# A graph layer with two feed-forward blocks: where a constant is added, which queue carries six stores, and what is done ahead of a branch

## The chip, the cores and the metric

The kernel runs on one core of a Trainium2 chip. The metric is the device time of one execution in microseconds. The core has five engines with an instruction stream each: TensorE (PE; its weight loads are shown as PEld), VectorE (DVE), ScalarE (ACT), GpSimd (POOL) and SyncE (SP), which here only issues transfers. Transfers are issued by SP, by POOL (all gathers, and in the change a few stores) and at the start by ACT. Engines and transfers wait for each other through semaphores.

## The reference

The input is x of 6250 nodes by 256, and 100,000 edges (src, dst), sorted by dst. Four residual blocks follow one another, each on the layer norm of x:

```python
x = x + gnn0(layernorm(x), W1, W2, b, src, dst)          # messages t1[src] + (f[src]*f[dst]) @ W2, summed by dst
x = x + ffn0(layernorm(x), wr, br, w1, b1, w2, b2)       # top half of the nodes by x @ wr gets gelu(x@w1+b1)@w2+b2, times that weight
x = x + gnn1(layernorm(x), edge_index, W, att_src, att_dst, bias, W_res, ...)
x = x + ffn1(layernorm(x), Wr, br, W1, b1, ..., Wo, bo)  # 8 experts of two layers with batch norm, all computed, mixed by a softmax
```

The change lies around gnn1, which is an attention over the edges into each node:

```python
xn = layer_norm(x, ln1_g, ln1_b)
h = (xn @ W).reshape(N, 8, 32)
e = leaky_relu((h*att_src).sum(-1)[src] + (h*att_dst).sum(-1)[dst], 0.2)
ee = exp(e - segment_max(e, dst)[dst]);  denom = segment_sum(ee, dst)
agg = segment_sum(h[src] * (ee / denom[dst])[:, :, None], dst)
out = layer_norm(agg + xn @ W_res + bias, ln2_g, ln2_b)
return out + gelu_tanh(out @ ffn_w1 + ffn_b1) @ ffn_w2 + ffn_b2
```

Adding out to x means adding (normed * ln2_g + ln2_b), and the ffn's bias ffn_b2 is a constant per column as well. The kernel holds ln2_b + ffn_b2 as one row, `cst`.

## The kernel before, in words

The 6250 nodes are 50 tiles of 125 rows (NT, NP). x stays in SBUF for the whole run as X. The edges of each tile, sorted by dst, are cut into slices of 128; each tile has 17 slices (SL) plus one place for the tile's own rows (the self loops), in three groups of six (GS, NG). The indices of all slices lie in sdT, as source rows (srcT) and as local destinations (dloc). A copy of the local destinations in DRAM, dltab, is read with a broadcast over the partitions to make the transposed one-hot matrices ohT (535.5 KB for a tile).

**First pass**, up to about 1246 us: gnn0 and ffn0, interleaved by generators. ffn0 (L519 to 545) works on chunks of four tiles (the last two chunks are of two and of one tile, 47, 48 and 49); each tile's result y goes from PSUM through DVE to SBUF and by `ndma` (L80 to 87, two transfers of 112 and 13 rows) to ytab in DRAM. L537 calls it. By the time of the last two chunks, `select` is at work: it finds the top half of the nodes by a search on DVE (L1342 to 1348), the routing. roots_of "rb" (rs, L178 to 185) makes the last reciprocal roots. On SP, the next transfer after the y stores is the load of h_w1 (L162), then h_w2, ohT0 (L680) and ten loads of Y, which bring ytab back (L85). They stand in this order in SP's stream.

**Between the passes.** For each tile, a list of steps (L784 to 792) does on staggered tiles: X += Y * wm (L784, DVE, both inputs in SBUF), norm to z (L742 on DVE for one tile in three, L744 on ACT), two transposes (L750), the gain (L754 on ACT, L755 on DVE), the product with W and the attention columns (L760) and the eviction (L777). Groups of five tiles are stored to htab, 264 columns wide: 256 of h and 8 attention terms. Then POOL gathers the rows of the first four groups of edges into a ring of four buffers, `ring` (fetch_edges, L699), by an indirect transfer per slice (L208). A loop over pairs of tiles (L848 to 865), here called the W_res loop, makes xn @ W_res, adds g_bias on DVE and stores rows to rtab, four tiles at a time. Among its steps, from t = 10 on, one step each of terms_by_parts (L829 to 845) builds adsh: the destination's attention term and its shift, split into three bf16 parts.

Then comes a branch (L866 to 880): a value is read from SBUF to all engines, and a general path is taken if the shifts are too far apart; with these inputs it is not taken. Every engine passes it.

**Second pass.** Its engines PE, DVE and ACT follow an order written out by hand, POOL and SP are ordered by the scheduler. Groups s = 0 to 149 (three a tile) go through four quarters:

- spread (L903): six matmuls of ohT with adsh give pa, the destination's terms per edge.
- quarter0 (L936): DVE reduces pa to ad and makes w (L941 to 945).
- quarter1 (L956): ACT takes exp of w into the group's rows (L959); DVE makes lo = rows − hi of the group before (L964).
- quarter2 (L966): fetch of a further group, spread of the next, and DVE multiplies the rows by the weights (L976, two halves).
- quarter3 (L978): PE sums rows by destination with the one-hot oh, in the two parts hi and lo (L986); ACT makes hi (L996), DVE makes oh (L998).

tile_end (L913) divides by the sum of weights and adds rr, the W_res row loaded from rtab (fetch_tile, L889 to 897, which also loads ohT of the tile; onehot_t, L899 to 901, compares it). own_rows (L691) loads the tile's own rows of htab.

The tiles are then taken in 14 chunks (1, 2, 3 and eleven times 4 tiles) through the norm, the ffn (up L1059, down L1070) and the experts (L1157, L1175, L1178). `run` shares the quarters of the next chunk's tiles out among the current chunk's matmuls. add_o (L1046 to 1053) is three POOL instructions for each chunk: o *= ln2_g, X += cst, X += o. The middle one needs nothing of the chunk but X as it is after L784, and in the trace all fourteen of it run between 1248 and 1317 us, among the products h.

The start of the second pass in the source (L1274 to 1284): fetch_tile(0), the own rows of the four ring buffers, the first experts' weights (`load`: W and Wo, L162), spread(0), then the quarters of the first chunk, among which fetch_tile(1) and fetch_tile(2) are called.

Of the kernel before, what the change touches and what calls it, by code (L numbers as in the profile page):

```python
# [9 lines left out]
F32 = mybir.dt.float32  # L10
# [4 lines left out]
ALU = mybir.AluOpType  # L15
# [45 lines left out]
def gnn_ffn(ctx, tc, A, out):  # L61
# [17 lines left out]
    def ndma(sb, tab, t0, load, eng=None):  # L79

        eng = eng or nc.sync
        view = tab[NP * t0:NP * (t0 + sb.shape[1]), :].rearrange("(t p) d -> p t d", p=NP)
        for a, b in ((0, SPLIT), (SPLIT, NP)):
            if load:
                eng.dma_start(sb[a:b], view[a:b])  # L85
            else:
                eng.dma_start(view[a:b], sb[a:b])
# [327 lines left out]
    with ExitStack() as p1:  # L415
# [103 lines left out]
        def ffn0(t0, c):  # L519
            xT = made.pop(t0)  # L520
            n = c * NP
            hT = []
            for f in range(NF):
                ph = psum.tile([P, CT * NP], F32, name="ph")
                for k in range(KD):
                    nc.tensor.matmul(ph[:, 0:n], f_w1[:, k, f * P:(f + 1) * P], xT[:, k, 0:n], start=(k == 0), stop=(k == KD - 1))  # L526
                h = late.tile([P, CT * NP], F32, name="hT", bufs=NF + 1)
                nc.scalar.activation(h[:, 0:n], ph[:, 0:n], AF.Gelu_apprx_tanh, bias=f_b1[:, f:f + 1])
                hT.append(h)
                yield  # L530
            for j in range(c):
                y = late.tile([NP, 1, D], F32, name="y")
                py = psum.tile([NP, D], F32, name="py", bufs=1)
                for f in range(NF):
                    nc.tensor.matmul(py, hT[f][:, j * NP:(j + 1) * NP], f_w2[:, f, :], start=(f == 0), stop=(f == NF - 1))  # L535
                nc.vector.tensor_tensor(y[:, 0, :], py, f_b2[0:NP, :], ALU.add)
                ndma(y, ytab, t0 + j, False)  # L537
                t = t0 + j
                x2 = late.tile([NP, D], F32, name="x2", bufs=1)
                nc.vector.scalar_tensor_tensor(x2, y[:, 0, :], wts[:, t:t + 1], X[:, t, :], op0=ALU.mult, op1=ALU.add)  # L540
                bn(late, mv2[:, 1, t, :], x2)
                yield
            if t0 < CHUNKS0[-2][0]:
                roots_of(t0, t0 + c, "ra")
# [166 lines left out]
    with ExitStack() as md:  # L711
# [133 lines left out]
                        nc.vector.tensor_tensor(rem[:, ts], rem[:, ts], adsh[0:NP, ts, q, :], ALU.subtract)  # L845


        rr = None  # L848
        made_terms = terms_by_parts()
        for t in range(0, NT, 2):  # L850
            pr = psum.tile([NP, 2, D], F32, name="pr")
            for i in range(2):
                for k in range(KD):
                    nc.tensor.matmul(pr[:, i, :], xTs[t + i][:, k, :], wcat[:, k, HA:HA + D], start=(k == 0), stop=(k == KD - 1))
            j = t % 4
            if j == 0:
                rr = pool.tile([NP, 4, D], F32, name="rr")
            nc.vector.tensor_tensor(rr[:, j:j + 2, :], pr, g_bias[0:NP, None, :].to_broadcast([NP, 2, D]), ALU.add)
            if j == 2 or t + 2 == NT:
                ndma(rr[:, 0:j + 2, :], rtab, t - j, False)  # L860
            if t >= 10:
                next(made_terms, None)
        for _ in made_terms:
            pass
        mid.close()
        gen1 = nc.values_load(f1I[0:1, 0:1], min_val=0, max_val=1)  # L866
        with tc.If(gen1 > 0):
# [14 lines left out]
    with ExitStack() as p2:  # L882
# [6 lines left out]
        def fetch_tile(t):  # L889
            if t >= NT:  # L890
                return
            ohT = ohT0 if t == 0 else pool.tile([NP + 1, SL, P], BF16, name="ohT")
            if t:
                nc.sync.dma_start(ohT.rearrange("p i e -> p (i e)"), flat_ap(dltab, t * SL * P, [[0, NP + 1], [1, SL * P]]))
            rr = pool.tile([NP, 1, D], F32, name="rr")
            ndma(rr, rtab, t, True)
            tiles[t] = {"ohT": ohT, "rr": rr}
# [37 lines left out]

        def quarter0(s):  # L936

            if s < LAST:
                L = live[s]
                ad = pool.tile([P, GS, 2 * HEADS], F32, name="ad")  # L940
                nc.vector.tensor_reduce(ad, L["pa"].rearrange("p i q c -> p i c q"), AX.X, ALU.add)  # L941
                w = pool.tile([P, GS, HEADS], F32, name="w")
                nc.vector.tensor_tensor(w, L["rows"][:, :, D:], ad[:, :, 0:HEADS], ALU.add)
                nc.vector.scalar_tensor_tensor(w, w, 0.2, w, op0=ALU.mult, op1=ALU.max)
                nc.vector.tensor_tensor(w, w, ad[:, :, HEADS:], ALU.subtract)
                L["w"] = w
            if s >= 2 and (s - 1) % NG == 0:
                tile_end((s - 1) // NG - 1)
            if s >= 2 and (s - 1) % NG == 0:
                fetch(s + len(ring) - 2)  # L950
            if s >= 1 and (s - 1) % NG == 0:
                fetch_tile((s - 1) // NG + 1)
            if s + 1 < LAST and (s + 1) % NG == 0:
                onehot_t((s + 1) // NG)

        def quarter1(s):  # L956

            if s < LAST:
                nc.scalar.activation(live[s]["rows"][:, :, D:], live[s].pop("w"), AF.Exp)  # L959
            if 1 <= s <= LAST:  # L960
                L = live[s - 1]
                L["lo"] = pool.tile([P, GS, HW], F32R, name="lo", bufs=1)
                for c in halves(real(s - 1)):
                    nc.vector.scalar_tensor_tensor(L["lo"][:, c], L["rows"][:, c], 1.0, L["hi"][:, c].bitcast(F32), op0=ALU.mult, op1=ALU.subtract)  # L964

        def quarter2(s):  # L966

            if s >= 1 and s % NG != 0:
                fetch(s + len(ring) - 1)
            if s + 1 < LAST:  # L970
                spread(s + 1)
            if s < LAST:
                rows = live[s]["rows"]
                for c in halves(GS):
                    h4 = rows[:, c, 0:D].rearrange("p i (h j) -> p i h j", j=HD)
                    nc.vector.tensor_tensor(h4, h4, rows[:, c, D:, None].to_broadcast([P, GS // 2, HEADS, HD]), ALU.mult)  # L976
# [69 lines left out]
        def add_o(ci):  # L1046

            t0, n = CHUNKS1[ci]
            o = outs.pop(ci)[0]
            bc = [NP, n, D]  # L1050
            nc.gpsimd.tensor_tensor(o[:, 0:n, :], o[:, 0:n, :], ln2_g[0:NP, None, :].to_broadcast(bc), ALU.mult)
            nc.gpsimd.tensor_tensor(X[:, t0:t0 + n, :], X[:, t0:t0 + n, :], cst[0:NP, None, :].to_broadcast(bc), ALU.add)
            nc.gpsimd.tensor_tensor(X[:, t0:t0 + n, :], X[:, t0:t0 + n, :], o[:, 0:n, :], ALU.add)

        def up(ci, f):
# [216 lines left out]
            return 4 * NG * (t0 + n) + 4  # L1272

        fetch_tile(0)  # L1274
        for k in range(len(ring)):
            own_rows(k)
        load(0, ("W1", "W2", "Wo"))
        load(1, ("W1", "W2"))
        spread(0)
        advance(ends(0))  # L1280
        for ci in range(len(CHUNKS1)):
            t0, n = CHUNKS1[ci]
# [426 lines left out]
```

## Time and profile before

| | |
|---|---|
| median of three runs | 3138.24 us (3135.61 to 3140.74) |
| profiled execution | 3140.49 us, its span 3138.7 us, mean TensorE clock 0.949 |
| TensorE busy | 2786.7 us, 89% of the span |
| VectorE, ScalarE, GpSimd busy | 2081.0, 1170.0 and 1964.4 us |
| transfers | 407.55 MB, 130 GB/s in the mean |

Where the time lies, by windows of the trace:

| stage | us from the span's start | length | PE busy | DVE busy | POOL busy |
|---|---|---|---|---|---|
| end of routing, first loads of Y | 1232 to 1248 | 16 | 3.4 | 12.1 | 0.6 |
| products h, 50 tiles | 1248 to 1323 | 75 | 66.5 | 63.3 | 31.1 |
| first gathers, W_res loop | 1323 to 1376 | 53 | 45.1 | 27.6 | 22.3 |
| branch passed, first groups | 1376 to 1394 | 18 | 7.2 | 14.6 | 9.9 |
| first chunks | 1394 to 1750 | 356 | 306.5 | 292.8 | 252.3 |
| chunks of four, the period repeats | 1750 to 3004 | 1254 | 1246.6 | 971.9 | 791.7 |
| last chunk | 3004 to 3138 | 134 | 128.0 | 28.2 | 4.7 |

How such a table is read: a share of busy time says which engine sets the pace of a stage only if it is near the whole. In other stages the rows in order of time tell more. Such a row has the start, the duration, the engine, the line, the operation, output and inputs, the shape, how many instructions it sums up, and in brackets the idle time ahead of it and what ended it. "SPq" is SP issuing transfers.

### The profile page before, as it was taken

What the parts mean: (1) busy time and instruction counts of PE and PEld (TensorE: products, weight loads), DVE (VectorE), ACT (ScalarE), POOL (GpSimd) and SP (SyncE); (2) the same over time, 40 slices, a digit from 0 to 9 for tenths busy, and PEclk for the clock granted to TensorE, in tenths of its full rate; (3) what the DMA queues carried; (4) which work ended last, traced back from release to release, by engine and by line L of the source; (5) the groups of instructions that cost most, each with busy time, mean ns of one, the idle gap of its engine ahead of it and who ended that gap; (6) DMA issues with size and microseconds to landing.
All of it is one profiled execution on the core that took longest, in us unless ns stands there. A gap on an engine that the chain in (4) does not pass through costs nothing.

```text
span 3138.7 us, 40435 instructions
## 1 busy us (share of the span) xinstructions
PE 2786.7 (89%) x12748; PEld 1981.1 (63%) x12748; DVE 2081.0 (66%) x5836; ACT 1170.0 (37%) x2149; POOL 1964.4 (63%) x1752
## 2 busy tenths in 40 slices
PE   4358888888888896867899999999999999999999
PEld 4345666666666675656776666666666666666665
DVE  7744555555555547767888777877877778787731
ACT  3302222222222222615545455354554545445332
POOL 4677777777777760456777666666666666666400
PEclk8778999999999997978999999999999999999999
DMA  5453343433333333465664545545455454544412
GB/s 124 100 150 102 113 115 112 112 112 112 112 112 113 112 105 90 134 189 166 189 168 137 166 135 144 154 127 163 131 155 146 134 163 123 162 139 136 128 50 61
DMA packets 262809, 407.55 MB, mean 130 GB/s; under 512 B 55312, under 2 KB 202236, under 8 KB 262543
## 3 DMA queue, kind: packets, MB, share of 16 engines
q0 software_dynamic: 80000, 221.18, 25.9%
q1 hardware_dynamic: 172765, 173.98, 18.9%
q10 hardware_dynamic: 9810, 9.60, 1.2%
q8 instruction: 106, 1.74, 0.2%
q14 instruction: 128, 1.05, 0.1%
HBM read 371.33 MB, written 34.04 MB: 129 GB/s over the span
## 4 chain that ended last, share of the span: by engine, by line
PE 47%; DVE 6%; ACT 1%; issue 1%; DMA 1%; POOL 0%; DVEq 0%; SPq 0%; ACTq 0%; POOLq 0%
PE ph L1157 19%; PE py L1175 9%; PE iotaP L986 5%; PE py L1070 5%; PE ph L1059 5%; DVE hrow L976 1%; PE mi L1032 1%; PE mi L1097 1%; DMA hrow<-htab,sdT 1%; DVE lo L964 1%; PE pa L909 1%; DVE oh L998 0%; DVE bnst L190 0%; POOL hrow L208 0%; ACT hi L996 0%
## 5 line engine op out<-in xcount | busy, mean ns | idle before, releaser
L208 POOL DMA_INDIRECT hrow<-htab,sdT x850 | 1017.2, 1197 | 527.6 <-issue 220.8
L208 POOL DMA_INDIRECT rows<-gtab,sdT x800 | 758.5, 948 | 243.6 <-issue 132.5
L1158 ACT ACTIVATE h<-ph,bi,sc 128x500 f32<-128x500 f32 (+3 forms) x448 | 321.5, 723 | 538.2 <-PE ph L1157 538.0
L455 PE MATMUL ps<-rows,oh 128*125 128x257 f32 x1600 | 429.8, 414 | 64.8 <-DMA rows<-gtab,sdT 49.1
L455 PEld LDWEIGHTS ps<-rows,oh 128*125 128x125 f32 x1600 | 313.3, 203 | 178.5 <-DMA rows<-gtab,sdT 83.8
L1157 PE MATMUL ph<-h,W 128*128 128x500 f32 (+3 forms) x896 | 372.0, 548 | 0.0
L1175 PE MATMUL py<-Wo,h 128*125 128x256 f32 x1600 | 369.8, 381 | 0.4 <-ACT h L1158 0.4
L1157 PE MATMUL ph<-wcat,W 128*128 128x500 f32 (+3 forms) x896 | 363.9, 545 | 2.4 <-ACT h L1158 2.3
L1175 PEld LDWEIGHTS py<-Wo,h 128*125 128x125 f32 x1600 | 296.7, 188 | 72.2 <-issue 27.9
L976 DVE TENSOR_TENSOR hrow<-hrow 128x768 f32<-128x768 f32 x300 | 280.1, 974 | 70.8 <-ACT hrow L959 70.8
L1178 DVE SCALAR_TENSOR_TENSOR X<-py,gate,X 125x256 f32<-125x256 f32 x400 | 173.4, 477 | 203.3 <-PE py L1175 203.2
L964 DVE SCALAR_TENSOR_TENSOR lo<-hrow,hi 128x792 fp32r<-128x792 f32 (+1 forms) x300 | 286.9, 997 | 0.2 <-issue 0.2
L996 ACT ACTIVATE hi<-hrow 128x792 fp32r<-128x792 f32 (+1 forms) x300 | 236.2, 822 | 127.0 <-DVE hrow L976 122.9
L986 PE MATMUL iotaP<-hi,oh 128*125 128x264 f32 x850 | 251.9, 329 | 0.0
L1157 PEld LDWEIGHTS ph<-wcat,W 128*128 128x128 f32 x896 | 160.8, 192 | 140.3 <-issue 109.8
L1157 PEld LDWEIGHTS ph<-h,W 128*128 128x128 f32 x896 | 160.0, 194 | 106.3 <-issue 95.8
L986 PE MATMUL iotaP<-lo,oh 128*125 128x264 f32 x850 | 219.5, 291 | 5.1 <-DVE lo L964 5.0
L1059 PE MATMUL ph<-xT,h_w 128*128 128x500 f32 (+3 forms) x448 | 185.9, 556 | 4.6 <-ACT hT L1061 3.6
L526 PE MATMUL ph<-xT,f_w 128*128 128x500 f32 (+3 forms) x448 | 185.6, 539 | 0.0
L535 PE MATMUL py<-f_w,hT 128*125 128x256 f32 x800 | 182.9, 381 | 0.9
L1070 PE MATMUL py<-h_w,hT 128*125 128x256 f32 x800 | 177.6, 380 | 0.0
L986 PEld LDWEIGHTS iotaP<-lo,oh 128*125 128x125 f32 x850 | 162.4, 191 | 20.8 <-issue 7.6
(355 smaller groups left out, 3929.7 us busy)
## 6 DMA issues: line engine op xcount, KB each, us to landing
W<-in_L_ffn_W SPq DMA_DIRECT2D x224, 256.0 KB
Wo<-in_L_ffn_Wo SPq DMA_DIRECT2D x112, 256.0 KB
ohT<-dltab SPq DMA_DIRECT2D x50, 535.5 KB
hrow<-htab,sdT POOLq DMA_INDIRECT x850
rows<-gtab,sdT POOLq DMA_INDIRECT x800
hrow<-htab SPq DMA_DIRECT2D x50, 115.5 KB
X<-in_x ACTq DMA_DIRECT2D x10, 560.0 KB
ytab<-y SPq DMA_DIRECT2D x50, 112.0 KB
```

The source lines that it names most:

```text
L208: nc.gpsimd.indirect_dma_start(out=dst, out_offset=None, in_=tab, in_offset=bass.IndirectOffsetOnAxis(ap=idx, axis=0))
L455: nc.tensor.matmul(ps, oh[:, i, :], edge_rows[i], start=(s0 + i == 0), stop=(s0 + i == SL - 1))
L526: nc.tensor.matmul(ph[:, 0:n], f_w1[:, k, f * P:(f + 1) * P], xT[:, k, 0:n], start=(k == 0), stop=(k == KD - 1))
L964: nc.vector.scalar_tensor_tensor(L["lo"][:, c], L["rows"][:, c], 1.0, L["hi"][:, c].bitcast(F32), op0=ALU.mult, op1=ALU.subtract)
L976: nc.vector.tensor_tensor(h4, h4, rows[:, c, D:, None].to_broadcast([P, GS // 2, HEADS, HD]), ALU.mult)
L986: nc.tensor.matmul(tiles[t]["ps"], L["oh"][:, i, :], r[:, i, :], start=(g + i + q == 0), stop=(g * GS + i == SL - 1 and q == 1))
L996: nc.scalar.activation(L["hi"][:, c], L["rows"][:, c], AF.Copy)
L1059: nc.tensor.matmul(ph[:, 0:n], h_w1[:, k, f * P:(f + 1) * P], C["xT"][:, k, 0:n], start=(k == 0), stop=(k == KD - 1))
L1070: nc.tensor.matmul(py[:, i, :], C["hT"][f][:, j * NP:(j + 1) * NP], h_w2[:, f, :], start=(f == 0), stop=(f == NF - 1))
L1157: nc.tensor.matmul(ph[:, 0:n], w[:, k, f * P:(f + 1) * P], rhs[:, k, 0:n], start=(k == 0), stop=(k == KD - 1))
L1158: nc.scalar.activation(h[:, f, 0:n], ph[:, 0:n], AF.Relu, bias=cols[1][:, f, e:e + 1], scale=cols[0][:, f, e:e + 1])
L1175: nc.tensor.matmul(py[:, i, :], hidden[u, "2"][:, k, j * NP:(j + 1) * NP], weights[u, "Wo"][:, k, :], start=(k == 0), stop=(k == KD - 1))
```

## The change

There are four parts.

1. The y stores of the last two chunks of ffn0, tiles 47, 48 and 49, six transfers, are issued by POOL rather than by SP.
2. In add_o, cst is added to o rather than to X. There are as many instructions of the same size, but the middle one now depends on the chunk's o. In the changed program the fourteen stand in POOL's stream in their chunks, behind o *= ln2_g, and X += o comes behind them, with a gather between each two.
3. Group 0 of the edges is spread, weighed and multiplied among the steps of the W_res loop (at t = 38, 42 and 46), ahead of the branch; the quarters of s = 0 skip these steps. The terms start one step sooner (t = 8), and none are left after the loop. The pa of group 0 takes one of the PSUM buffers "mi".
4. fetch_tile(1) follows fetch_tile(0), ahead of the own rows and of the weights on SP, rather than in the first quarters.

```diff
-                ndma(y, ytab, t0 + j, False)
+                ndma(y, ytab, t0 + j, False, eng=nc.gpsimd if t0 >= CHUNKS0[-2][0] else None)
...
+        def spread_first():
+            pa = psum.tile([P, GS, 3, 2 * HEADS], F32, name="mi", bufs=3)
+            for i in range(GS):
+                nc.tensor.matmul(pa[:, i].rearrange("p q c -> p (q c)"), ohT0[:, i, :], adsh[:, 0].rearrange("p q c -> p (q c)"),
+                                 start=True, stop=True)
+            hts["pa"] = pa
+
+        def weigh_first():
+            rows = ring[0]
+            ad = wp.tile([P, GS, 2 * HEADS], F32, name="ad0")
+            nc.vector.tensor_reduce(ad, hts.pop("pa").rearrange("p i q c -> p i c q"), AX.X, ALU.add)
+            w = wp.tile([P, GS, HEADS], F32, name="w0")
+            nc.vector.tensor_tensor(w, rows[:, :, D:], ad[:, :, 0:HEADS], ALU.add)
+            nc.vector.scalar_tensor_tensor(w, w, 0.2, w, op0=ALU.mult, op1=ALU.max)
+            nc.vector.tensor_tensor(w, w, ad[:, :, HEADS:], ALU.subtract)
+            nc.scalar.activation(rows[:, :, D:], w, AF.Exp)
+
+        def multiply_first():
+            rows = ring[0]
+            for c in (slice(0, GS // 2), slice(GS // 2, GS)):
+                h4 = rows[:, c, 0:D].rearrange("p i (h j) -> p i h j", j=HD)
+                nc.vector.tensor_tensor(h4, h4, rows[:, c, D:, None].to_broadcast([P, GS // 2, HEADS, HD]), ALU.mult)
+
+        firsts1 = {38: spread_first, 42: weigh_first, 46: multiply_first}
...
-            if t >= 10:
+            if t >= 8:
                 next(made_terms, None)
-        for _ in made_terms:
-            pass
+            if t in firsts1:
+                firsts1[t]()
+        assert next(made_terms, 0) == 0
...
-            if s < LAST:
+            if 0 < s < LAST:
                 L = live[s]
                 ad = pool.tile([P, GS, 2 * HEADS], F32, name="ad")
...
-            if s < LAST:
+            if 0 < s < LAST:
                 nc.scalar.activation(live[s]["rows"][:, :, D:], live[s].pop("w"), AF.Exp)
...
-            if s < LAST:
+            if 0 < s < LAST:
                 rows = live[s]["rows"]
...
-            if s >= 1 and (s - 1) % NG == 0:
+            if s > 1 and (s - 1) % NG == 0:
                 fetch_tile((s - 1) // NG + 1)
...
-            nc.gpsimd.tensor_tensor(X[:, t0:t0 + n, :], X[:, t0:t0 + n, :], cst[0:NP, None, :].to_broadcast(bc), ALU.add)
+            nc.gpsimd.tensor_tensor(o[:, 0:n, :], o[:, 0:n, :], cst[0:NP, None, :].to_broadcast(bc), ALU.add)
...
         fetch_tile(0)
+        fetch_tile(1)
         for k in range(len(ring)):
             own_rows(k)
         load(0, ("W1", "W2", "Wo"))
         load(1, ("W1", "W2"))
-        spread(0)
         advance(ends(0))
```

## The prediction

> **What bounds the kernel now.** I read the page's busy shares first, then its forty slices, then busy time by stage (windows cut where the slices change), and last the time-ordered rows, with their idle times, at the four places that the change touches. The profiled execution took 3140.49 us for a span of 3138.7, 1.8 us outside the span, and lies 2.25 us above the median of the three runs (3138.24). The sum below is a difference; I set it against the median. What a measurement of this kernel can tell from no change is about 0.2%, 6.3 us.
>
> ```profile
> PE 2786.7 (89%) x12748; PEld 1981.1 (63%) x12748; DVE 2081.0 (66%) x5836; ACT 1170.0 (37%) x2149; POOL 1964.4 (63%) x1752
> ...
> 1248.00:1323.00 75.00, 66.47 (x300) 50.10 (x300) 63.26 (x135) 52.25 (x133) 31.08 (x14) 0.88 0.55 144
> 1323.00:1376.00 53.00, 45.07 (x215) 38.25 (x216) 27.58 (x60) 1.28 (x1) 22.34 (x23) 0.99 0.66 189
> 1376.00:1394.00 18.00, 7.16 (x36) 6.09 (x36) 14.64 (x24) 5.63 (x9) 9.90 (x8) 0.50 0.86 226
> ...
> 1750.00:2550.00 800.00, 795.02 (x3589) 528.56 (x3588) 624.07 (x1349) 387.85 (x605) 522.68 (x420) 1.00 0.51 145
> 2550.00:3004.00 454.00, 451.55 (x2027) 300.00 (x2027) 347.81 (x755) 214.52 (x337) 268.97 (x217) 1.00 0.49 137
> ```
>
> The window rows give start and end, length, busy time (count) of PE, PEld, DVE, ACT and POOL, then clock, DMA share and GB/s. From 1750 on TensorE works 99.4% of the time at full clock: nothing is gained there, anything that makes PE wait is lost, and an earlier start is carried to the end. 1376 to 1394, the start of the second pass, is a chain of waits: PE 7.16 us of 18, clock 0.50. Between lie the products h (1248 to 1323) and W_res (1323 to 1376).
>
> **The part that costs most now: the fourteen X+=cst.** In the source they belong to add_o, but the scheduler has put them between the steps of the h products. The groups of 1247 to 1323 by shape:
>
> ```profile
> L784 DVE SCALAR_TENSOR_TENSOR X<-Y,wm,X 125x256 f32<-125x256 f32 x50 | 39.5, 798 | 0.0
> L1052 POOL TENSOR_TENSOR X<-X,cst 125x1024 f32<-125x1024 f32 x11 | 26.8, 2433 | 37.1 <-DVE z L742 17.9 <-ACT z L744 15.1 <-DVE X L784 4.1
> ```
>
> Eleven of four tiles take 26.8 us of POOL, the three smaller 1.9, 1.4 and 1.0. L784, with both inputs in SBUF, lasts 474 ns in the median and up to 2423 beside one of them: 39.5 − 50 x 0.474 = 15.8 us stretched. What of that is on the path? The tiles come every 1.137 us where nothing disturbs (eight tiles from 1276.44 to 1285.52); tiles 14 to 49 take 1276.44 to 1322.38 = 45.94 us against 34 x 1.137 + 0.65 = 39.3. At most 6.6 us can go, at least the 3 of the plainest gaps; I take 5.9. The next limit is PE, which paces the 1.137. Nothing is won ahead of 1270, since this wait for a store stays:
>
> ```profile
> 1269.94 0.40 ACT L777 ACTIVATE ht<-ph 125x272 f32<-125x272 f32 x1 [4.55 <-DMA htab<-ht]
> ```
>
> The W_res loop behind it is paced by PE (1.73 us for two tiles), so the 5.9 pass through. **−5.9 (−6.6 to −3).**
>
> **The same fourteen as o+=cst, in the chunks.** They now stand on POOL between o*g and X+=o, with gathers between. Chunk 4 before, POOL and then DVE:
>
> ```profile
> 1802.49 2.69 POOL L1051 TENSOR_TENSOR o<-o,ln_g 125x1024 f32<-125x1024 f32 x1 [4.15 <-PE mi L1032]
> 1805.34 1.55 POOL L208 DMA_INDIRECT hrow<-htab,sdT  x1 [0.15 <-issue]
> 1806.91 2.39 POOL L1053 TENSOR_TENSOR X<-X,o 125x1024 f32<-125x1024 f32 x1
> ```
> ```profile
> 1802.00 4.03 DVE L964 SCALAR_TENSOR_TENSOR lo<-hrow,hi 128x792 fp32r<-128x792 f32 x2
> 1808.42 2.58 DVE L976 TENSOR_TENSOR hrow<-hrow 128x768 f32<-128x768 f32 x2 [2.39 <-ACT hrow L959]
> 1810.92 0.93 DVE L998 SCALAR_TENSOR_TENSOR oh<-sdT,iota 128x750 fp32r<-128x750 f32 x1
> ...
> 1813.56 1.87 DVE L964 SCALAR_TENSOR_TENSOR lo<-hrow,hi 128x792 fp32r<-128x792 f32 x2
> ```
>
> Beside o*g the pair of lo takes 4.03 instead of 1.87; that is as before. The new op takes the slot of X+=o (1806.91), and X+=o moves behind one more gather, to 1806.91 + 2.39 + 0.16 + 1.51 = about 1811.0, upon oh at 1810.92. By the stretch of lo, oh or the small w behind it ends 2.1 us later; so does the first half of the next lo, ready at 1813.56 + 0.94 + 2.1 = 1816.6. PE takes up its first lo matmul at 1816.33 and loses the pair's start-up, some 0.45 us in all with the refill I allow (0 if DVE gives way less, 0.9 if both ops hit lo). Afterwards DVE has idle gaps (1.29 at 1821.8, 4.80 ahead of X at 1828.4), X+=o is done 15 us before that X is read, and the gathers' queue has 3.7 us idle at 1833.7. Nine chunks (4 to 12) repeat this period of 133.6 us; the last, at 3004, has no gathers beside it. 9 x 0.45 = **+4.0 (0 to +8).**
>
> The Trainium skill ("SBUF — State Buffer", Who interferes with whom) says that of a two-input DVE op and a GpSimd op that reads SBUF, the one issued first holds the shared ports until it is through. The rows agree for lo; for the new place the rule would let oh (ahead by 0.07 us) pass and block the w ops until about 1814.3, lo's first half would be there at 1816.5 and PE lose 0.2 instead of 0.45, which would make the sum −6.8. No row of before has X+=o there, so I keep the 0.45.
>
> **The first four chunks** get the additional 0.73, 1.30, 1.9 and 2.35 us on POOL while its gathers set much of the pace (1444 to 1750: POOL 222 of 306 us busy, PE 275). DVE waits for py of L1070 there for 4.5 to 5.5 us a chunk, which covers X+=o being late; what remains is gathers 6.3 us later over 300 us. I take a quarter, **+1.5 (−1 to +4.5)**.
>
> **Start of the second pass.** Before:
>
> ```profile
> 1374.53 0.38 PE L909 MATMUL pa<-adsh,ohT 126*128 126x48 bf16 x6 [5.01 <-DVEq L867]
> 1375.00 0.46 DVE L941 TENSOR_REDUCE ad<-pa 128x96 f32<-128x288 f32 x1 [4.16 <-PE pa L909]
> ...
> 1376.49 1.83 DVE L976 TENSOR_TENSOR hrow<-hrow 128x768 f32<-128x768 f32 x2 [0.31 <-ACT hrow L959]
> 1377.48 1.73 ACT L996 ACTIVATE hi<-hrow 128x792 fp32r<-128x792 f32 x2 [1.02 <-DMA rr<-rtab]
> ...
> 1388.66 0.79 DVE L901 TENSOR_SCALAR ohT<-ohT,pcol 126x2176 bf16<-126x2176 bf16 x1 [2.59 <-DMA ohT<-dltab]
> ```
>
> pa, ad, w, exp and the multiply of group 0 now precede the branch. hi can begin when ACT is past it, about 1375.7 (SP, which passes last, issues its first load at 1375.68). lo of group 0 and the multiply of group 1 move from 1380.46 and 1382.25 to about 1377.9 and 1379.6: −2.6; the gather that waits for lo (1381.71) follows. Then the chain would stand at ohT of tile 1, which landed at 1388.6, 7.8 us after its issue at 1380.79. The change issues it after two rr loads only, about 1376.5, so it lands near 1382; the 2.59 of waiting go as well, and about half a microsecond comes back through the own rows, which now go out 1.35 us later behind 535 KB. That makes **−4.7 (−5.2 to −1)**. W and Wo, pushed behind, are first used at 1429.58.
>
> What precedes the branch has to be paid in the W_res loop: six matmuls, 0.38 to 0.45 us on PE; on DVE ad 0.46, three w at 0.21 and the multiply 1.83. DVE has 1.03 us to spare in each step of the loop, so only the last step but one is late. Queued behind ad and w are the evictions of pr, for which PE waits only at the second one. The last rr store already waits 1.63 us for an earlier store. I take **+0.6 (0.4 to 2)**. The terms that begin one step sooner (t = 8) fit into the same slack: nothing, and if they did not, 0.93 us once (L842).
>
> **The six y stores of tiles 47 to 49 on POOL.** POOL is idle 62.6 us there, up to 1231.46. SP's next load waits for these stores and also for the last DVE step of roots_of (L185, 1231.19 to 1231.35), in both kernels:
>
> ```profile
> 1231.42 0.93 SPq L162 DMA_DIRECT2D h_w<-in_L_gnn_ffn_w  x2
> ```
>
> The last y leaves DVE at 1222.4. Even with two issues of 1.4 us (the dear gathers of this trace) and 3 us of landing, it is there by 1228.2 (an allowance: the 535 KB of ohT took 7.8 us with full queues; these 128 KB meet a DMA share of 0.04, window 1180 to 1232). So nothing starts sooner and nothing later: **0**; the cover is 3 us, and what goes beyond delays the Y loads one for one until the wait of 4.55 us at 1269.94 takes it up in part. The Trainium skill ("DMA: Bandwidth & Descriptors", SWDGE vs HWDGE) gives about 1 us to the first byte for DMAs that GpSimd generates and 0.6 from SyncE's queue; that speaks against the move, but by it the stores end 0.4 us later, under the same cover, and the sum stays.
>
> **Sum:** −5.9 − 4.7 + 4.0 + 1.5 + 0.6 = −4.5 us, 3138.24 − 4.5 = 3133.7. All good ends together: −6.6 − 5.2 − 1 + 0.4 = −12.4, 3125.8; all bad ones: −3 − 1 + 8 + 4.5 + 2 = +10.5, 3148.7.
>
> **Rivals.** (A) The o+=cst cost PE nothing, because DVE's lead over PE takes up the delay (its gaps speak for that; that lo's first half is only 1.8 us ahead of its matmul speaks against): −4.5 − 4.0 = −8.5, 3129.7. (B) Slower side: X+=o upon oh and the w ops delays exp, hi and the next lo as well, and PE waits twice a chunk. All else is −8.5, so above 0.95 us a chunk nothing is left; at 1.3 us, three times my stall, it is −8.5 + 11.7 = +3.2, 3141.4, and beyond 1.65 us it is measurably slower. That lo was stretched 2.16 us without PE waiting more than 0.3 speaks against. (C) The change of the start does not do what it says: hi(0) and the loads still wait for the last rtab store at the join, so only 1.5 of the 4.7 come: −1.3, 3136.9. For: idle 5.01 at the branch now; against: ACT had nothing else to wait for but the multiply. (D) Stores from POOL land after 1231.35 and push the Y loads, by 2 to 3 us: 3136.
>
> **How the numbers follow.** Forecast's case 0.41 (3131 to 3137), A 0.30, B 0.13, C 0.11, D 0.05. Faster by over 0.2% (under 3131.96) are most of A and the low edge of the forecast's: 0.24 + 0.11 = 0.35. Slower by over 0.2% (above 3144.5): half of B and the joint bad ends, 0.09. The rest, 0.56, is within 0.2%. The range leaves out a tenth on each side: from the good ends, 3126, to the middle of B with a bad ramp, 3143.
>
> **What would show it.** Right: no X<-X,cst on POOL between 1247 and 1323, L784 at 474 ns mean, the h loop some 6 us shorter; hi of group 0 about 1.8 us nearer to the branch; the wait for ohT of tile 1 gone; from 1750 on PE waits "<-DVE lo" of some 4 us in the whole. Wrong: h tiles still further apart than 1.14 us; PE below 99% in the windows from 1750 on; h_w1 issued at another time relative to L185.

## The result, and the profile after

The changed kernel takes 3151.18 us (median of six runs, 3146.77 to 3153.11), the kernel before 3138.41 beside it (3134.36 to 3140.74, six runs). The ratio is 1.0042 with a 95% interval of 1.0031 to 1.0054: slower by 0.42%, some 13 us. The forecast was 3133.7 us, with a range up to 3143.

Set side by side, the two profiled executions (spans 3151.2 and 3138.7 us) show where that comes from. Each row is a difference between starts of instructions, read from the rows in order of time.

| stage | before | after | difference |
|---|---|---|---|
| first to last eviction of the products h | 69.77 | 63.80 | −5.97 |
| to the first eviction of the W_res loop | 5.03 | 6.17 | +1.14 |
| W_res loop, first to last eviction | 42.74 | 45.13 | +2.39 |
| to tile_end of tile 0 | 29.13 | 23.96 | −5.17 |
| to the store of chunk 0's result | 109.91 | 111.29 | +1.38 |
| chunks 1, 2 and 3, store to store | 352.30 | 357.47 | +5.17 |
| chunks 4 to 11 | 1068.79 | 1082.82 | +14.03 |
| chunks 12 and 13 | 203.79 | 203.84 | +0.05 |

The first pass is the same (h_w1 issued at 1231.42 and 1231.49). The gains of the h products and of the start came as large as forecast, and by the store of chunk 3 all but 1.1 us of them is used up. The ffn of a chunk begins before the store of the one ahead (add_o of chunk 4 stands at 1802, the store of chunk 3 at 1861), so chunks 4 to 12 of the prediction are the stages 3 to 11 of this table. Each of these loses some 1.75 us: the period is 135.35 us instead of 133.6. The waits of TensorE from 1750 to 3000, of the changed kernel and then of the kernel before:

```profile
PE pa L935 <- DVE ohT L927: 13.8, 9, 1.5
PE mi L1058 <- DVE z L1108: 6.9, 9, 0.8
```
```profile
PE mi L1032 <- DVE z L1082: 7.0, 9, 0.8
```

The numbers are microseconds in all, times, the longest. The wait for z was there before; the first line is new. TensorE waits 1.5 us for ohT in each of nine chunks. The same chunk as in the prediction, after: first POOL, then DVE, then PE.

```profile
1799.33 2.67 POOL L1077 TENSOR_TENSOR o<-o,ln_g 125x1024 f32<-125x1024 f32 x1 [4.18 <-PE mi L1058]
1803.73 2.38 POOL L1078 TENSOR_TENSOR o<-o,cst 125x1024 f32<-125x1024 f32 x1
1807.80 2.35 POOL L1079 TENSOR_TENSOR X<-X,o 125x1024 f32<-125x1024 f32 x1
```
```profile
1798.82 4.03 DVE L990 SCALAR_TENSOR_TENSOR lo<-hrow,hi 128x792 fp32r<-128x792 f32 x2
1805.25 2.56 DVE L1002 TENSOR_TENSOR hrow<-hrow 128x768 f32<-128x768 f32 x2 [2.41 <-ACT hrow L985]
1807.73 3.23 DVE L1024 SCALAR_TENSOR_TENSOR oh<-sdT,iota 128x750 fp32r<-128x750 f32 x1
1810.88 0.45 DVE L967 TENSOR_REDUCE ad<-pa 128x96 f32<-128x288 f32 x1
...
1811.97 0.78 DVE L927 TENSOR_SCALAR ohT<-ohT,pcol 126x2176 bf16<-126x2176 bf16 x1
1812.66 1.87 DVE L990 SCALAR_TENSOR_TENSOR lo<-hrow,hi 128x792 fp32r<-128x792 f32 x2
```
```profile
1812.80 0.32 PE L935 MATMUL pa<-adsh,ohT 126*128 126x48 bf16 x6 [1.53 <-DVE ohT L927]
```

X += o starts 0.07 us behind oh, just as the multiply ahead of oh ends (1805.25 + 2.56 = 1807.81), and oh lasts 3.23 us instead of 0.93. All that follows on DVE is 2.3 us later, and the first to feel it is the spread (pa), not the matmuls of lo. The chain of work that ended last goes the same way in this chunk: o*g on POOL, the gather, the multiply, oh (3.15 us of it), ad, w, ohT, pa.

At the h products the groups answer to the two lines of before: there is no X<-X,cst on POOL, and L784 has come down from 798 to 478 ns.

```profile
L784 DVE SCALAR_TENSOR_TENSOR X<-Y,wm,X 125x256 f32<-125x256 f32 x50 | 23.5, 478 | 0.0
```

At the start of the second pass ohT of tile 1 is there when DVE comes to it. Its compare starts at 1380.65 with no idle time before it, and hi of group 0 at 1372.15, as soon as the branch is passed:

```profile
1372.15 1.62 ACT L1022 ACTIVATE hi<-hrow 128x792 fp32r<-128x792 f32 x2 [8.57 <-SPq L893]
```

### The profile page after: what moved, and what is told of

Read it like the earlier page. It is cut to its first block, busy times and chain, and to the rows that moved or that the text cites. A ratio compares the mean times of both kernels' runs of the same rounds, so it can differ in the third digit from the quotient of the medians.

```text
span 3151.2 us, 40415 instructions
## 1 busy us (share of the span) xinstructions
PE 2794.5 (89%) x12748; PEld 1984.8 (63%) x12748; DVE 2092.1 (66%) x5836; ACT 1170.1 (37%) x2149; POOL 1966.8 (62%) x1758
## 4 chain that ended last, share of the span: by engine, by line
PE 43%; DVE 8%; DMA 2%; ACT 1%; issue 1%; POOL 1%; DVEq 0%; ACTq 0%; POOLq 0%
PE ph L1183 19%; PE py L1201 9%; PE py L1096 5%; PE iotaP L1012 5%; PE ph L1085 2%; DVE hrow L1002 2%; DMA hrow<-htab,sdT 2%; DVE oh L1024 1%; PE mi L1058 1%; DVE lo L990 1%; PE mi L1123 1%; PE pa L935 1%; DVE ohT L927 1%; DVE bnst L190 0%; POOL o L1077 0%
```

## The experiments

Each group below ran on one chip, beside runs of the kernel before on that chip, and ratios are to those runs. In the groups of e5 to e8 and of e13 to e16 the first pass took 1640 to 1657 us instead of 1231, for every kernel, and the kernel before 3575 to 3577 us. Why is not known. There, only the ratios are of use, and the stages behind the first pass when they are compared within the group (with no X += cst beside it, the W_res loop takes 61 to 65 us there and 42 to 45 in the others).

| run | what it is | ratio to before, 95% interval |
|---|---|---|
| e1_add_only | before, o += cst alone | 1.0040 (1.0027 to 1.0053) |
| e2_rest_only | the change without o += cst | 1.0008 (0.9999 to 1.0017) |
| e3_oht_sooner | the change, ohT ahead of oh | 1.0018 (1.0009 to 1.0027) |
| e4_cst_wres | the change, X += cst in one run beside the W_res loop | 1.0062 (1.0043 to 1.0080) |
| e5_no_cst | before, no cst | 0.9984 (0.9972 to 0.9997) |
| e6, e14_fetch_only | before, fetch_tile(1) sooner | 0.9997 (0.9985 to 1.0009), 0.9992 (0.9977 to 1.0008) |
| e7, e15_first_only | before, first group ahead of the branch | 1.0013 (1.0000 to 1.0027), 1.0012 (1.0000 to 1.0023) |
| e8_cst_between | before, X += cst between the gathers | 0.9957 (0.9943 to 0.9971) |
| e10_between_all | the same, all fourteen | 1.0014 (1.0005 to 1.0023) |
| e11_between_fetch | e10 with fetch_tile(1) sooner | 1.0029 (1.0019 to 1.0039) |
| e12_after_between | the change, X += cst between the gathers | 1.0031 (1.0020 to 1.0043) |
| e16, e17_cst_single | before, X += cst tile by tile | 0.9991 (0.9977 to 1.0004), 0.9978 (0.9970 to 0.9987) |
| e18_after_single | the change, X += cst tile by tile | 0.9986 (0.9978 to 0.9995) |

### Is it o += cst? One part alone, and all the others

My theory after the result: o += cst pushes X += o behind one more gather and upon oh; ohT ends late, and the spread waits. The first rival: the slower period comes from the other parts, which shift the second pass against the gathers. The edit of e1 to the kernel before (e2 is the changed kernel with the same line turned back):

```diff
-            nc.gpsimd.tensor_tensor(X[:, t0:t0 + n, :], X[:, t0:t0 + n, :], cst[0:NP, None, :].to_broadcast(bc), ALU.add)
+            nc.gpsimd.tensor_tensor(o[:, 0:n, :], o[:, 0:n, :], cst[0:NP, None, :].to_broadcast(bc), ALU.add)
```

> The kernel before with one line changed: add_o adds cst to o, not to X; the y stores, the first group and fetch_tile stay as they were. Theory 1 (the X+=o that is pushed behind one more gather falls on oh, so that onehot_t ends late and TensorE's spread waits for it): the h products end some 6 us sooner, each chunk of four takes 135.3 us instead of 133.6, TensorE waits for ohT about 1.5 us in each of 9 chunks; in all +12 to +16 us, near 3152. Theory 2 (the slower period comes from the other parts, which shift the second pass against the gathers): no wait for ohT, a period of 133.6, only the gain of the h products, near 3133.

> The changed kernel with the one line of add_o put back (X += cst); stores on POOL, first group ahead of the branch, fetch_tile(1) sooner and the terms from t = 8 stay. Theory 1: the fourteen instructions are among the h products again, the period is 133.6 us, no wait for ohT, and what is left is the gain at the start of the second pass less what the W_res loop loses, -1 to -5 us: near 3135. Theory 2: the period stays at 135.3 us and the time near 3150.

e1 alone is as slow as the whole change: 3151.10 against 3139.67 us. Its period is 135.3 us, and its waits from 1750 to 3000 hold the new one:

```profile
PE pa L909 <- DVE ohT L901: 13.9, 9, 1.6
```

In e2 this wait is missing, oh takes 0.93 us, and the period is 133.66. The rival falls. But e2 is not 1 to 5 us faster, as I expected; it is at +0.08%, with an interval from no change to +0.17%. That became the second question.

### Is it the place of ohT, or the 2.4 us of POOL?

Second rival: the additional POOL time delays the gathers, and TensorE pays for it wherever it happens to wait. e3 leaves POOL as it is and moves one instruction of DVE, from the second tile on:

```diff
-            if s + 1 < LAST and (s + 1) % NG == 0:
-                onehot_t((s + 1) // NG)
+            if s + 1 == NG:
+                onehot_t(1)
...
+                if s + 2 < LAST and s > 1 and (s + 2) % NG == 0:
+                    onehot_t((s + 2) // NG)
                 L["oh"] = pool.tile([P, GS, NP], F32R, name="oh")
```

> The changed kernel, but from the second tile on the comparison of ohT (onehot_t) stands ahead of oh in VectorE's order and not behind the w of the next group. The POOL instructions and their places stay. Theory 1: oh still takes about 3.2 us beside X += o, but the spread no longer waits for ohT; what remains is at most the small wait for lo that the prediction worked out (0.45 us a chunk), so 9 to 14 us come back: 3138 to 3142. Theory 3 (the additional 2.4 us of POOL a chunk delay the gathers, and TensorE pays for that wherever it waits): the wait moves to another instruction, and the time stays near 3150.

```profile
1804.39 2.54 DVE L1002 TENSOR_TENSOR hrow<-hrow 128x768 f32<-128x768 f32 x2 [2.42 <-ACT hrow L985]
1806.86 3.02 DVE L927 TENSOR_SCALAR ohT<-ohT,pcol 126x2176 bf16<-126x2176 bf16 x1
1809.80 0.93 DVE L1026 SCALAR_TENSOR_TENSOR oh<-sdT,iota 128x750 fp32r<-128x750 f32 x1
```
```profile
1811.14 0.31 PE L935 MATMUL pa<-adsh,ohT 126*128 126x48 bf16 x6 [0.73 <-DVE ad L967]
```

The period falls from 135.35 to 134.53, the ratio from 1.0042 to 1.0018. TensorE no longer waits for ohT, so the order on DVE decides, and not POOL's total. But only 0.82 of the 1.75 us come back, and of the 9 to 14 us expected some 6 (3145.13 us, against 3151.10 of e1 on the same chip). X += o (1806.93 to 1809.28) now holds up ohT itself, 3.02 us instead of 0.78, although that instruction has one input. ad now starts 6.26 us behind the start of the multiply, where it was 3.35 in the kernel before, and as there is one pa buffer, the spread waits 0.73 us for ad to have read it. Both expectations were too simple; the mechanism of theory 1 stands, with a second victim behind the first.

### What the hoisted X += cst cost, and whether it can be placed better

e4 puts the eleven large instructions behind the first gathers, in one run, where POOL is idle; VectorE adds cst to the first six tiles. e5 leaves cst out.

```diff
         for k in range(len(ring)):
             fetch_edges(k)
+        for t0, n in CHUNKS1[3:]:
+            nc.gpsimd.tensor_tensor(X[:, t0:t0 + n, :], X[:, t0:t0 + n, :], cst[0:NP, None, :].to_broadcast([NP, n, D]), ALU.add)
```

> The changed kernel with cst added to X neither in the chunks nor among the h products: for the eleven chunks of four tiles POOL adds it behind its first 23 gathers, beside the W_res loop, where it is idle for 27.8 us; for the first six tiles VectorE adds it among the first three steps of that loop. Theory 1: the h products run undisturbed, the period is 133.6 us, and the loop loses 1 to 3 us where the instructions meet the terms, the w and the multiply of the first group; near 3133 (3131 to 3136). Theory 2: the period stays at 135.3 us, near 3148.

> The kernel before without the fourteen instructions of cst: ln2_b + ffn_b2 is not added to X, all else is as before, the order of the other instructions too. It measures what the fourteen cost among the h products. Theory A (an earlier start is carried to the end): the h products end 6 to 10 us sooner, the period stays at 133.6, and the time falls by as much, to about 3132. Theory B (a stage between gives it back, the W_res loop or the first chunks, where the clock dips): sooner at the h products, but less than 3 us are left at the end, 3136 to 3138.

e4 is the slowest of all, 3158.97 us, and its rows, DVE and then POOL, give the reason:

```profile
1349.86 0.68 DVE L885 TENSOR_TENSOR rr<-pr,g_bias 125x512 f32<-125x512 f32 x1
1350.46 25.49 DVE L847 TENSOR_TENSOR rem<-rem,adsh 125x752 f32<-125x752 f32 x1
```
```profile
1349.82 25.33 POOL L795 TENSOR_TENSOR X<-X,cst 125x1024 f32<-125x1024 f32 x11
```

One DVE instruction of 0.93 us waited for eleven POOL instructions on end; TensorE stood for 25 us. I had expected the loop to lose 1 to 3 us. A hold over several instructions is not the rule, though. In the kernel before, in chunk 2, o*g ends at 1557.97 and X += o starts at 1558.06; lo, which starts at 1557.98, keeps its 0.97 us, and X += o takes 2.56 us, where o*g of the same size takes 1.81. In e17 below, instructions on one tile stand on end with no gap between them, and no L784 beside them lasts more than 0.95 us. What sets e4 apart stays open. The period in e4 is 133.66, as theory 1 had it.

e5 is 0.16% faster than before (0.03 to 0.28%): some 6 us, by the interval 1 to 10, is what the fourteen cost among the h products. Next, the same instructions with a gather between each two of them; e8 has thirteen of the fourteen (cst is not added to the last four tiles), e10 all.

```diff
             if g * GS + i < SL:
                 gather(live[s]["rows"][:, i, :], htab, srcT[:, t, g * GS + i:g * GS + i + 1])
+                if between and (s or i >= 3) and i % 3 != 2:
+                    between()
```

> The kernel before with the fourteen X += cst neither among the h products nor behind the gathers in one run, but each between two of the first 23 gathers on POOL (from 1325 to about 1381 us). If VectorE is let through whenever POOL turns to a gather, each of its two-input instructions of the W_res loop (rem -= adsh) waits for one POOL instruction at most, 2.4 us, and four such meetings cost TensorE 0 to 4 us in the loop; the h products gain 6 to 10 us, the period stays at 133.6: near 3134. If a gather does not end the hold, rem -= adsh waits for the whole row of instructions as in the kernel that has them in one run, and the time is near 3155.

> The kernel before with all fourteen X += cst put between the first gathers on POOL, two for each three gathers. Expected: the h products 4 to 7 us shorter, each meeting of a two-input VectorE instruction with X += cst costs at most one POOL instruction, the W_res loop 0 to 4 us longer, the period 133.6; in all -1 to -6 us. If the W_res loop gives all of it back, 0 to +3.

> The same with fetch_tile(1) ahead of the own rows and the weights as in the changed kernel. Expected: 1 to 2.6 us less than without it, if the earlier ohT of tile 1 is carried through chunk 0; the same time, if chunk 0 gives it back.

> The changed kernel with X += cst between the first gathers in place of o += cst in the chunks; stores on POOL, first group ahead of the branch and fetch_tile(1) stay. Expected if the whole loss came from o += cst: 12 to 18 us less than the changed kernel, -1 to -6 us against the kernel before. The w and the multiply of the first group meet the last X += cst, which may take 2 to 5 us of it back.

The gathers do end the hold, but in the W_res loop most two-input DVE instructions of the terms, and one copy, meet one. Groups of e10, 1314 to 1372:

```profile
L854 DVE TENSOR_TENSOR rem<-rem,adsh 125x752 f32<-125x752 f32 x2 | 5.9, 2960 | 0.0
L854 DVE TENSOR_TENSOR rem<-rem,adsh 125x48 f32<-125x48 f32 x2 | 4.2, 2125 | 0.0
L834 DVE SCALAR_TENSOR_TENSOR rem<-shift 125x376 f32<-125x376 f32 x1 | 3.3, 3272 | 0.0
L848 DVE COPY rem<-ASAD 125x376 f32<-125x376 f32 x1 | 2.9, 2915 | 0.0
```

In e9 (the kernel before, profiled on the same chip) these four take 0.93, 0.20, 0.58 and 0.35 us. The loop takes 53.85 us instead of the 42.39 of e9, which gives back more than the h products gained (60.71 us instead of 66.29). e8's 0.43% is no contradiction: in its group the loop took 62 to 65 us in the other kernels, and it is 52.6 in e8. I do not count it. e11 and e12 are no faster than e10, and e12, expected 12 to 18 us below the changed kernel, is by the ratios some 3 us below it (its loop takes 57.84 us).

e16 and e17 leave the instructions among the h products and cut them to single tiles:

```diff
-            nc.gpsimd.tensor_tensor(X[:, t0:t0 + n, :], X[:, t0:t0 + n, :], cst[0:NP, None, :].to_broadcast(bc), ALU.add)
+            for t in range(t0, t0 + n):
+                nc.gpsimd.tensor_tensor(X[:, t, :], X[:, t, :], cst[0:NP, :], ALU.add)
```

> The kernel before with X += cst as fifty instructions of one tile (about 0.65 us each) in place of fourteen of up to four tiles; they stay among the h products. If the cost there comes from the length of one hold (2.4 us, twice the 1.14 us between two tiles), VectorE's waits become shorter than the buffers between the steps, the h products take 60 to 64 us and the time falls by 2 to 6 us. If it comes from the sum of the holds, the h products stay at 66 to 70 us or grow, and the time stays or rises by up to 5 us.

> The kernel before with X += cst as fifty instructions of one tile. Where the first pass takes 1231 us: h products 58 to 62 us, all other stages as before, the end 5 to 10 us sooner than before (ratio 0.997 to 0.9985). If the h products gave it back later, the ratio is 0.999 or more.

```profile
L1053 POOL TENSOR_TENSOR X<-X,cst 125x256 f32<-125x256 f32 x50 | 43.0, 875 | 31.4 <-ACT z L744 21.6 <-DVE z L742 9.6
...
L784 DVE SCALAR_TENSOR_TENSOR X<-Y,wm,X 125x256 f32<-125x256 f32 x50 | 26.2, 531 | 0.0
```

The groups are of e17. POOL works longer (43.0 us instead of 31.1), but L784 has 531 ns instead of 798, and the h products take 58.2 us, against 66.3 to 69.8 in the three profiles of before (58.1 in e16, against 69.2 of before in its group). So it was the length of one hold, longer than the 1.14 us between two tiles, and not their sum. e17 is the fastest kernel of this study: 3130.33 us against 3136.43, 0.9978 (0.9970 to 0.9987), faster than both kernels. e16's ratio shows no such gain (0.9977 to 1.0004); its profile has the longest first pass of all (1657 us), but that this hides the gain is not shown.

### Where the gain at the start of the second pass went

e6 and e14 move fetch_tile(1) alone, e7 and e15 the first group alone; e9 and e13 are the kernel before once more, for the stages.

> The kernel before with only fetch_tile(1) moved ahead of the own rows and the weights. Theory A: the wait of VectorE for ohT of tile 1 (2.59 us) goes, tile_end(0) comes 1 to 2.6 us sooner, and so does the end, near 3137. Theory B: tile_end(0) comes sooner, but TensorE starts chunk 0 at the lower clock and the end stays within 1 us of before.

> The kernel before with only the first group spread, weighed and multiplied ahead of the branch, and the terms from t = 8. Theory A: the loop over W_res loses 0.4 to 2 us, tile_end(0) gains about 2.6 from the branch on; at the end -2 to 0 us. Theory B: nothing is left at the end, or a loss of 1 to 2 us.

> The kernel before, unchanged, profiled once more beside the next three kernels, so that stages are compared on the same chip. If the W_res loop and chunk 0 take 44 us and 111 us here too (42.7 and 109.9 in the first profile), the 1 to 2 us that kernels with the changed start lost in these stages is no effect of the change; if they take 42.7 and 109.9, it is.

> The kernel before, unchanged, for the stages on the chip of the next three kernels: first h product to last, last h product to first rr, W_res loop, last rr to tile_end(0), tile_end(0) to the store of chunk 0. On two chips these were 66 to 70, 5.0, 42.4 to 42.7, 28.8 to 29.1 and 109.9 to 110.2 us.

> The kernel before with only fetch_tile(1) moved ahead of the own rows and the weights. Theory A (the gain is real and carried on): last rr to tile_end(0) 1 to 2.6 us shorter, chunk 0 the same, the end 1 to 2.6 us sooner. Theory B (chunk 0 gives it back, because TensorE's clock rises with its own work and not with the time at which it may begin): chunk 0 longer by as much, the end within 1 us.

> The kernel before with only the first group ahead of the branch and the terms from t = 8. Theory A: last rr to tile_end(0) 2.6 us shorter, the W_res loop 0.4 to 1 us longer, the end 1 to 2 us sooner. Theory B: the loop 1.4 to 2.4 us longer, or chunk 0 or the periods longer, and the end 0 to 4 us later.

> The changed kernel with X += cst as fifty instructions of one tile in place of o += cst; stores on POOL, first group ahead of the branch, fetch_tile(1) and the terms from t = 8 stay. If the start of the second pass is carried to the end, 3 to 5 us less than the kernel with the fifty instructions alone; if the W_res loop and the clock give it back, the same time or up to 3 us more. Either way 10 us or more below the changed kernel as it is.

The gain is there at its place: from the last eviction of the loop to tile_end(0) the six kernels with both parts need 23.6 to 24.1 us, the fourteen without both 27.1 to 30.7. It takes both. With fetch_tile(1) alone the stretch takes 27.1 us against 28.0 (e14 and e13), and neither e6 nor e14 differs in time from before. With the first group alone, the next wait grows, DVE's for ohT of tile 1, from 1.40 us in e13 to this one in e15:

```profile
1830.25 0.79 DVE L927 TENSOR_SCALAR ohT<-ohT,pcol 126x2176 bf16<-126x2176 bf16 x1 [6.68 <-DMA ohT<-dltab]
```

The first group has a price far ahead of its place. The loads of Y, and the wait of the h products for a store behind them, in e13 and then e15, whose instructions up to there are the same:

```profile
1649.12 27.03 SPq L85 DMA_DIRECT2D Y<-ytab  x22
...
1685.17 0.40 ACT L777 ACTIVATE ht<-ph 125x272 f32<-125x272 f32 x1 [3.99 <-DMA htab<-ht]
```
```profile
1654.81 28.58 SPq L85 DMA_DIRECT2D Y<-ytab  x22
...
1692.74 0.40 ACT L777 ACTIVATE ht<-ph 125x272 f32<-125x272 f32 x1 [6.34 <-DMA htab<-ht]
```

In all eight kernels with the first group the 22 loads take 28.2 to 29.6 us to issue, at 228 to 244 GB/s, and the store wait is 5.4 to 7.2 us. In all twelve without it they take 25.8 to 27.8 us at 246 to 275 GB/s, and the wait is 1.95 to 4.55. The means of the wait are 6.0 and 3.2 us. (The rates are those of 20 us, from 9 us behind the issue of h_w1.) With y stores on POOL or without makes no difference (e7 and e15 have none there). What else differs in this stretch is the room that is taken in SBUF: the two small tiles of weigh_first, 576 bytes of each partition, come out of the same pool as Y. That Y lies elsewhere for it, and that this slows the loads, is only a guess: the traces show no addresses, and no run has moved Y alone. The cause stays open.

So some 2.9 us of the 5.2 are lost there. The W_res loop is 1.2 us longer with the first group in one pair (e15 against e13) and 0.5 us shorter in another (e7 against e6). Where o += cst is absent, the period is 133.66 with it and 133.60 without, 0.5 us over the chunks. e18 against e17 puts the whole of these parts, once o += cst is out of the way, at 2.35 us slower (3132.68 and 3130.33; the intervals overlap); e2 said the same. That they gain nothing is shown; the last 2 us of it are within what these runs can tell.

## Why the prediction was wrong

**What failed.** It is the step of the o += cst in the chunks, +4.0 us with a range of 0 to 8. Measured: 14.0 us over the stages 4 to 11 and 1.8 in stage 3, 15.8 in all. Of the 17 us between the forecast of −4.5 and the result of +12.8, this step makes 11.8. The cause and the place were right. X += o was put at oh's start plus 0.08 us and came at plus 0.07; the stretch was put at 2.1 us and is 2.30. But the text then followed the delay to the first half of lo alone, which has 1.8 us to spare, and got 0.45 us. Between oh and lo stands ohT, and its reader, the spread, stands ahead of the lo matmuls on TensorE. In the trace of before, DVE and then PE:

```profile
1812.86 0.78 DVE L901 TENSOR_SCALAR ohT<-ohT,pcol 126x2176 bf16<-126x2176 bf16 x1
```
```profile
1814.29 0.31 PE L909 MATMUL pa<-adsh,ohT 126*128 126x48 bf16 x6
```

ohT ends at 1813.64 and the spread starts at 1814.29: 0.65 us to spare. 2.30 − 0.65 = 1.65 is what TensorE must wait; 1.53 was measured, and the period grew by 1.75. Every number for this lay in rows that I had before me. The error was to check the consumer I had in mind, and not each instruction behind the delayed one.

**The rivals.** B had the sign, the cause and the point from which it decides ("beyond 1.65 us it is measurably slower"; measured 1.75). Its path was wrong as well: exp, hi and lo, where it was ohT. I gave it 0.13, because lo had been stretched by 2.16 us "without PE waiting more than 0.3". That was lo beside o*g, with no ohT behind it: another place in the period, with another reader. A fell with these nine waits, C with the −5.17 at the start, D with h_w1, which is issued as early as before.

**What the skill's rule said.** The prediction weighed the rule of the Trainium skill, "SBUF — State Buffer", Who interferes with whom, that whoever issues first holds the shared ports until it is through. Read by the start times, oh, ahead by 0.07 us, would have passed untouched; it was held for 2.30 us. But so short a lead proves little, as the multiply ahead of oh is over only at 1807.81, 0.01 us behind the start of X += o. With a longer lead the rule fits: the first half of lo, 0.51 us ahead of o*g, keeps its 0.98 us, and o*g takes 2.67 us instead of the 2.35 that it takes with no DVE beside it (at 3017.02). With a lead of under 0.1 us the start times do not tell who is held: lo in chunk 2 of before, 0.08 us ahead, was not. What the same section says of tensor_scalar, that it can enter a mode that uses the shared ports, fits e3: ohT, a bf16 tensor_scalar with one input, went from 0.78 to 3.02 us.

**h products, −5.9.** −5.97 in the pair of profiles; e5 prices it at −6 us in total time (−1 to −10). The mechanism was right; that the size agrees so well is luck in part. The stage spreads from 66.3 to 69.8 us in three profiles of before. The wait for a store, which the prediction left as it was, grew from 4.55 to 5.45 us in this pair, and e1, where it is 3.93, has 59.58 us, 10.2 less than before.

**First chunks, +1.5 (−1 to +4.5).** Chunks 1 and 2 grew by 0.2 and 3.15 us, and so they did in e1: 3.4 us together, within the range. Chunk 0's 1.4 us says nothing: that stage takes 108.4 to 112.2 us, in kernels with and without the edit.

**Start of the second pass, −4.7.** −5.17, and for the reasons given: the first group off the path, then ohT of tile 1. What was missed is that the part has a price elsewhere, at the loads of Y, for which the prediction has no term.

**W_res loop, +0.6.** +2.39, and +1.14 ahead of it. This is not the first group: e1, which lacks it, has 44.34 and 6.18. The windows of the changed kernel show the clock (the column before the last two):

```profile
1320.00:1324.00 4.00, 4.00 (x13) 3.17 (x12) 1.26 (x5) 0.00 (x0) 3.09 (x4) 0.58 0.24 68
1324.00:1328.00 4.00, 4.00 (x20) 3.50 (x19) 1.38 (x2) 0.00 (x0) 3.09 (x4) 1.00 0.70 178
```

TensorE does 13 matmuls in the first 4 us and 20 in the next. Before, the clock was 1.00 from 1318 to the end of this stretch; there it dipped earlier, to 0.67 from 1314 to 1318, within the products h. So the two stages are better read together with the step between them: −2.4 us in all. The step ahead of the loop takes 6.0 to 7.0 us instead of 5.0 in nine of the twenty profiles, with and without each part of the change; all nine with the short first pass; what sets it off stays open.

**The y stores on POOL, 0.** Right: h_w1 is issued right after the last step of roots_of in both kernels.

## What to carry to other kernels

When an instruction is delayed, list every later instruction of its engine up to the one you have in mind, with its first reader and the time that reader has to spare; the smallest of these decides. Elementwise work on GpSimd beside a busy VectorE was priced here by the length of one instruction against the slack of the pipeline beside it, so cut it into pieces shorter than a step (fifty pieces cost less here than fourteen, with 12 us more of work), and where several stand on end, look in the trace whether VectorE gets in between (in e4 it did not). A stage that is full at 99% turns a small stall into a loss per period, so an edit that moves work there has to win its price times the number of periods.

## What was not expected of the hardware

- A VectorE instruction of 0.93 us waited 24.6 us while eleven GpSimd instructions ran on end (e4). Elsewhere VectorE got in between two of them: lo at 1557.98 of the kernel before, L784 in e17. With a gather in between, instructions last 2 to 3 us (e10).
- Of two instructions that start within 0.1 us of each other, the start times do not tell which is held: oh, 0.07 us ahead, was (0.93 to 3.23 us), lo, 0.08 us ahead, was not (0.97 us). One-input instructions were held too: a bf16 tensor_scalar (0.78 to 3.02 us, e3) and an f32 copy (0.35 to 2.92 us, e10).
- X += cst on one tile takes 0.72 us at the least and 0.88 in the mean (e17), on four tiles 2.35 and 2.43 (before).
- The loads of Y ran at 228 to 244 GB/s in the eight kernels with the first group's two small tiles, at 246 to 275 in the other twelve. Why stays open.
